# Sums of a softmax's terms: eight blocks on GpSimd, two chains of transfers, no block alone

## The chip, the cores and the metric

The kernel runs on one core of a Trainium2 chip. The metric is the device time of one execution in microseconds (us); smaller is better. A core has engines that run side by side, each working through its own list of instructions in order: TensorE (PE in the profile) multiplies matrices, VectorE (DVE) and ScalarE (ACT) work element by element, GpSimd (POOL) does too and also issues transfers (DMA) that can add to their destination, and SyncE (SP) issues plain transfers. They wait for each other through semaphores. TensorE writes into PSUM; the other tiles here lie in SBUF, or in DRAM.

## The reference

The input is x, 8 images of 2048 tokens with 256 channels, and an adjacency matrix of 2048 x 2048. A graph attention layer with 8 heads of 32 channels is followed by normalizations and a small two-layer network:

```
scores = einsum('fnhd,fmhd->fhnm', q, k) / sqrt(D)
scores = where(adj > 0, scores, -1e9)
attn   = softmax(scores, axis=-1)
t      = einsum('fhnm,fmhd->fnhd', attn, v)
x1 = layernorm(x + t);  x2 = layernorm(x1 + relu(x1 @ w1 + b1) @ w2 + b2)
out = layernorm(x + x2)
```

For every query and head the softmax needs one denominator, the sum of exp(score) over the 2048 keys. How that sum is formed is what the change is about.

## The kernel before

The attention is tiled by image f (8), chunk qc of 512 queries (4), half g of the heads (2 halves of 4 heads), and block mb of 128 keys (16). One (f, qc, g) is a **group**; there are 64, counted from 0 in this text, so an image has eight. One block is an **item**, 1024 in all, and the main loop has one **step** per item.

For an item, `scores` makes the products of keys and queries on PE (line 223) in PSUM, DVE adds the mask and writes the tile `p` (line 226), and ACT takes the exponential in place (line 228). A tile `p` has 128 keys on its partitions and 4 heads x 512 queries along its rows, 1 MB. `values` multiplies it with the values on PE (line 240), summing over the group's 16 blocks in PSUM.

The denominators need a sum over all keys, across the 16 tiles and across the partitions. The partitions are summed by a product with a matrix of ones on PE in `denominator` (line 294), four products, one for each head, per tile: a *set*. To have fewer sets, tiles are first added to each other in `add_up`, called after `values` in each step:

- the blocks of `POOLED` are added on GpSimd into the first of them (line 260);
- the blocks of each chain in `MOVED` are added into the chain's first by a transfer that accumulates, issued by GpSimd (line 257). Each such transfer reads and writes the chain's first tile and so waits for the one before it in its chain;
- the block `ALONE` is added to nothing.

Then `denominator` makes a set for each remaining tile (four), all into one PSUM bank, copies the sum to SBUF on ACT as `dT` (line 296), turns it on PE (line 301) and takes the reciprocal on DVE. Before line 301 the copy has to be done, and ACT gets to it in the order of its list.

The tiles `p` come from a pool of 10 buffers (`bufs=10`). A tile's buffer is free after its last reader: the add or transfer that consumes it, or for a chain's first the ones-products. A buffer freed longest ago is the next to be taken.

The order of the work is written out by hand; nothing is reordered by a planner. In step t the loop first calls `advance`, then issues the scores of item t+2 (`LEAD` is 2), then values and `add_up` of item t:

```
if mb:
    advance(t, 1)
...
    scores(items[t + LEAD])
values(items[t])
add_up(items[t])
if mb == LAST:
    start(t + SUM, denominator(f, qc, g), t)
```

`advance` runs the other work, held as generators in a list sorted by a due time; each `yield BANK` needs a free PSUM bank, and one bank is given per step (none at block 0). `denominator` starts `SUM` = 4 steps after its group's last block, that is in block 3's step of the next group. It has a `yield BANK` before its first set and another one ahead of the set n == 2, so that sets 0 and 1 are made in block 3's step and the rest in block 4's. After that come the turn of dT and, for g = 1, the output's tail (`outcome`, `tail`): normalizations (`norm`, with four small operations on POOL, lines 271 to 275, and four on ACT, line 278), the two-layer network (lines 352 and 362), four adds and multiplications of the whole tile on POOL (lines 344, 346, 367, 369), and two accumulating transfers of x issued by POOL (lines 328 and 371).

POOL's list holds, in this order within a step: the tail's operations that `advance` issues, and then the step's add or transfer.

Of the kernel before, what the change touches and what calls it, by code (L numbers as in the profile page):

```python
# [20 lines left out]
D = 32  # L21
# [32 lines left out]
def fast_path(ctx, tc, cst, x, adj, out, RS):  # L54
    nc = tc.nc
# [29 lines left out]
    def bank(dt=F32):  # L85
        shape = [P, CH] if dt == F32 else [P, 2, CH]
        if state["side"] is not None:
            i = 1 - state["side"]
            return ps_x[i].tile(shape, dt, name=f"x{i}")
        i = state["turn"]  # L90
        state["turn"] = (i + 1) % 5
        pool = ps_s[i] if i < 3 else ps_x[i - 3]
        return pool.tile(shape, dt, name=f"s{i}" if i < 3 else f"x{i - 3}")
# [119 lines left out]
    PT, O, OT, RC = {}, {}, {}, {}  # L213
# [31 lines left out]

    POOLED = (0, 3, 6, 8, 11, 13, 15)
    MOVED = ((1, 4, 7, 10), (2, 5, 9, 12))
    ALONE = 14  # L250
    SUM = 4

    def add_up(item):
        f, qc, g, mb = item
        for chain in MOVED:
            if mb in chain[1:]:
                nc.gpsimd.dma_start(PT[f, qc, g, chain[0]], PT.pop(item), accum_op=ALU.add)  # L257
        if mb in POOLED[1:]:
            first = PT[f, qc, g, POOLED[0]]
            nc.gpsimd.tensor_tensor(first, first, PT.pop(item), ALU.add)  # L260
# [22 lines left out]

    def denominator(f, qc, g):
        grp = (f, qc, g)
        terms = [PT.pop((f, qc, g, ALONE))] + [PT.pop((f, qc, g, chain[0])) for chain in MOVED + (POOLED,)]
        yield BANK
        ps = bank()
        for n, term in enumerate(terms):
            if n == 2:  # L290
                yield BANK
            for h in range(4):
                r = D * h
                nc.tensor.matmul(ps[r:r + D, :], cst["ones"], term[:, h, :], start=(n == 0), stop=(n == 3))  # L294
        dT = op.tile([P, CH], F32, name="dT")
        nc.scalar.copy(dT, ps)
        yield 1
        yield BANK
        ps = bank()
        for j in range(TPC):  # L300
            nc.tensor.transpose(ps[:, j * P:(j + 1) * P], dT[:, j::TPC], ident)
        if g == 0:
            RC[f, qc] = op.tile([P, TPC, H], F32, name="rc")
        rc = RC[f, qc]
        den = ps.rearrange("p (j c) -> p j c", c=P)[:, :, ::D]
        nc.vector.reciprocal(rc[:, :, 4 * g:4 * g + 4], den)
        nc.vector.tensor_tensor(RS[:, 0], RS[:, 0], den, ALU.add)
        nc.vector.tensor_tensor(RS[:, 1], RS[:, 1], den, ALU.min)
        if g == 1:
            begin = items.index((f, qc, g, LAST)) + SUM + 2  # L310
            start(begin, outcome(f, qc), begin)

    def outcome(f, qc):
        yield ROOM
        state["tails"] += 1
        rc = RC.pop((f, qc))
        xin = x[f, qc * CH:(qc + 1) * CH, :].rearrange("(p j) c -> p j c", p=P)
        y = yp.tile([P, TPC, C], F32, name="y")
        for gg in range(2):
            oT = OT.pop((f, qc, gg))  # L320
            yield BANK
            ps = bank()
            for j in range(TPC):
                nc.tensor.transpose(ps[:, j * P:(j + 1) * P], oT[:, j::TPC], ident)
            nc.vector.tensor_tensor(y[:, :, gg * P:(gg + 1) * P].rearrange("p j (h d) -> p j h d", d=D),
                                    ps.rearrange("p (j h d) -> p j h d", h=4, d=D),
                                    rc[:, :, 4 * gg:4 * gg + 4, None].to_broadcast([P, TPC, 4, D]), ALU.mult)
        nc.gpsimd.dma_start(y, xin, accum_op=ALU.add)
        begin = items.index((f, qc, 1, LAST)) + SUM + 2
        start(begin + 10, tail(f, qc, y, xin), begin + 26)  # L330
# [49 lines left out]
    def start(t, gen, due):  # L380
        fill.append([t, gen, 1, due])
        fill.sort(key=lambda e: e[3])
# [72 lines left out]
    for t, (f, qc, g, mb) in enumerate(items):  # L455
        if mb == 0 and t:
            state["side"] = 1 - state["side"]
        if f == 0 and g == 0 and mb == 0 and qc + 1 < NCK:
            start(t, mask_ahead(qc + 1), t + 28)
        if g == 1 and mb == 0 and (f or qc == NCK - 1) and (f + 1 < F or qc + 1 < NCK):  # L460
            load_mask(f + (qc + 1) // NCK, (qc + 1) % NCK)
        if f + 1 < F:
            for what, *which in NEXT.get((2 * qc + g, mb), []):
                due = t + MB // 2 if what is turn else items.index((f + 1, 0, which[1], which[0] * TPC)) - LEAD - 1
                start(t, what(f + 1, *which), due)
        if mb:
            advance(t, 1)
        if t + LEAD < len(items):
            nf, _, ng, nmb = items[t + LEAD]
            t0 = t  # L470
            while (nf, nmb // TPC, ng) not in V:
                advance(t0, 1)
                t0 += 1
# [5 lines that stand above are left out]
# [129 lines left out]
def kernel(  # L608
# [56 lines left out]
    nc.gpsimd.memset(RS[:, 1], 1.0)  # L665

    fast_path(tc, cst, x, adj, out, RS)


# [49 lines left out]
```

## Time and profile before

| | us |
|---|---|
| median of 3 runs | 3730.4 (3729.24 to 3743.26) |
| the profiled execution's own time | 3733.92 |
| its span, first to last instruction | 3732.1 |
| PE busy | 3241.8 (87%) |
| DVE busy | 2760.8 (74%) |
| POOL busy | 2599.1 (70%) |
| ACT busy | 2411.0 (65%) |
| 16 DMA engines, GpSimd's queue | 58.1% of the span |

Line numbers (L294) are those of the kernel before. In lists of groups a row gives line, engine, operation, output<-inputs, how often, then the busy time in all, the mean of one in ns, the idle time of the engine just before it and what ended that. In the timeline a row gives the start, the length, engine, line, operation, and in brackets the idle time before it with what ended it. A matrix product in f32 leaves two records, so a set of four products leaves 8. A POOL record often overlaps the next one's start.

### The profile page before, as it was taken

How to read it: one execution, taken by the hardware profiler on the slowest of the kernel's cores; microseconds unless marked ns; L12 is line 12 of the kernel's file. 1: busy time of each engine (PE TensorE's matmuls, PEld its weight loads, DVE VectorE, ACT ScalarE, POOL GpSimd, SP SyncE). 2: the span in 40 equal slices, each digit the busy share in tenths (PEclk: the TensorE clock that was granted, in tenths of full speed). 3: DMA queues.
4: the chain of work that ended last, by engine and by line, in shares of the span. 5: the costliest groups of instructions: out<-in, count | busy, mean ns of one | idle time of the engine just before them, and what ended most of it. 6: DMA issues, size and time to landing. Idle time of an engine off the chain costs nothing. (4 is left out here: it accounts for less than half of the span.)

```text
span 3732.1 us, 53786 instructions
## 1 busy us (share of the span) xinstructions
PE 3241.8 (87%) x22020; PEld 1038.8 (28%) x22020; DVE 2760.8 (74%) x3203; ACT 2411.0 (65%) x1921; POOL 2599.1 (70%) x1363
## 2 busy tenths in 40 slices
PE   7877888899988899889998899889898889988884
PEld 4222223222322233222332223222232222322221
DVE  4777766877688766788677777777768877688883
ACT  3554555766667666766666776666666676677663
POOL 2555666777677775877667785777777777687775
PEclk9998999999999999999999999999999999999997
DMA  6766675776766775776766776676676676676664
GB/s 185 175 142 152 146 175 117 168 162 142 173 150 145 158 171 145 169 153 154 169 138 151 163 172 158 140 165 154 147 175 141 148 171 152 154 164 140 139 134 86
DMA packets 113774, 573.31 MB, mean 154 GB/s; under 512 B 10833, under 2 KB 27729, under 8 KB 60273
## 3 DMA queue, kind: packets, MB, share of 16 engines
q0 software_dynamic: 64848, 436.90, 58.1%
q1 hardware_dynamic: 47856, 131.61, 10.0%
q8 instruction: 174, 2.85, 0.3%
q10 hardware_dynamic: 816, 1.31, 0.1%
q14 instruction: 80, 0.65, 0.0%
HBM read 129.37 MB, written 37.75 MB: 45 GB/s over the span
## 5 line engine op out<-in xcount | busy, mean ns | idle before, releaser
L226 DVE TENSOR_TENSOR p<-s,mask 128x1024 f32<-128x1024 f32 x2048 | 2410.3, 1219 | 753.8 <-PE s L223 480.0
L228 ACT ACTIVATE p<-p 128x2048 f32<-128x2048 f32 x1024 | 1957.1, 1911 | 1232.9 <-DVE p L226 916.2
L260 POOL TENSOR_TENSOR p<-p 128x2048 f32<-128x2048 f32 x384 | 1835.9, 4810 | 653.6 <-ACT p L228 645.0
L223 PE MATMUL s<-qT,kT 32*128 32x512 f32 x8192 | 1193.2, 652 | 232.5 <-DVE p L226 231.0
L240 PE MATMUL x<-p,v 128*32 128x512 f32 x8192 | 1112.2, 616 | 0.0
L257 POOL DMA_DIRECT2D p<-p x384 | 382.7, 1018 | 351.2 <-ACT p L228 138.9
L223 PEld LDWEIGHTS s<-qT,kT 32*128 32x128 f32 x8192 | 325.3, 186 | 853.6 <-DVE p L226 695.6
L240 PEld LDWEIGHTS x<-p,v 128*32 128x32 f32 x8192 | 162.3, 108 | 795.2 <-issue 645.1
L180 PE MATMUL x<-in,wqkv 128*128 128x512 f32 x472 | 234.6, 620 | 23.1 <-ACT oT L244 10.2
L278 ACT ACTIVATE y<-y,nb,rs 128x256 f32<-128x256 f32 x384 | 224.9, 589 | 38.0 <-POOL nb L275 38.0
L294 PE MATMUL x<-p,ones 128*32 128x512 f32 x2048 | 246.3, 599 | 1.8 <-DVE y L364 0.9
L267 DVE BATCH_NORM_STATS2 st<-y 128x6 f32<-128x256 f32 x384 | 160.1, 417 | 27.1 <-DMA y<-in_x_dram 27.1
L362 PE MATMUL x<-w2s,hT 128*128 128x256 f32 x512 | 127.6, 392 | 45.7 <-ACT oT L244 42.3
L352 PE MATMUL x<-turned,w1s 128*128 128x512 f32 x256 | 128.8, 626 | 20.8 <-ACT hT L353 19.5
L180 PEld LDWEIGHTS x<-in,wqkv 128*128 128x128 f32 x472 | 80.3, 190 | 186.1 <-issue 69.8
L362 PEld LDWEIGHTS x<-w2s,hT 128*128 128x128 f32 x512 | 92.1, 190 | 112.0 <-ACT oT L244 68.6
L205 PE MATMUL x<-wqkv,in 128*128 128x128 f32 x896 | 114.9, 282 | 6.4 <-ACT kT L182 6.3
L205 PEld LDWEIGHTS x<-wqkv,in 128*128 128x128 f32 x896 | 104.2, 192 | 55.0 <-ACT kT L182 34.0
L364 DVE TENSOR_TENSOR y<-x,y 128x512 f32<-128x512 f32 x64 | 44.3, 692 | 94.9 <-PE x L362 94.7
L294 PEld LDWEIGHTS x<-p,ones 128*32 128x32 f32 x2048 | 64.0, 111 | 165.8 <-issue 129.7
L272 POOL TENSOR_TENSOR rs<-rs,mhalf 128x4 f32<-128x4 f32 x96 | 99.3, 1035 | 8.0
L341 PE MATMUL x<-ident,y 128*128 128x128 f32 x256 | 48.0, 299 | 54.5 <-ACT turned L342 38.8
(87 smaller groups left out, 1427.1 us busy)
## 6 DMA issues: line engine op xcount, KB each, us to landing
p<-p POOLq DMA_DIRECT2D x384, 1024.0 KB, 9.7
y<-in_x_dram POOLq DMA_DIRECT2D x64, 512.0 KB, 6.1
in<-xd SPq DMA_DIRECT2D x59, 512.0 KB, 8.0
mask<-md SPq DMA_DIRECT2D x28, 1024.0 KB, 6.6
out_dram<-y SPq DMA_DIRECT2D x32, 512.0 KB, 3.0
in<-in_x_dram SPq DMA_DIRECT2D x28, 512.0 KB, 6.9
xd<-in SPq DMA_DIRECT2D x28, 512.0 KB, 10.0
in<-in_adj_dram SPq DMA_DIRECT2D x24, 512.0 KB, 7.6
```

The lines of the kernel that those rows point to most:

```text
L180: nc.tensor.matmul(ps, wqkv[:, a, k0:k0 + P], xT[:, a, :], start=(a == 0), stop=(a == 1))
L205: nc.tensor.matmul(ps[:, j * P:(j + 1) * P], xT[:, a, j * P:(j + 1) * P], wqkv[:, a, 2 * C + g * P:2 * C + (g + 1) * P], start=(a == 0), s ...
L223: nc.tensor.matmul(ps2[half][:, j, :], KT[f, mb // TPC, g][r:r + D, (mb % TPC) * P:(mb % TPC + 1) * P], QT[f, qc, g][r:r + D, :], start=Tr ...
L226: nc.vector.tensor_tensor(pt[:, 2 * half:2 * half + 2, :], ps, MK[f, qc][:, mb, None, :].to_broadcast([P, 2, CH]), ALU.add)
L228: nc.scalar.activation(pt, pt, AF.Exp, scale=1.0 / math.sqrt(D))
L240: nc.tensor.matmul(O[grp][r:r + D, :], V[f, mb // TPC, g][:, mb % TPC, r:r + D], PT[item][:, h, :], start=(mb == 0), stop=(mb == LAST))
L257: nc.gpsimd.dma_start(PT[f, qc, g, chain[0]], PT.pop(item), accum_op=ALU.add)
L260: nc.gpsimd.tensor_tensor(first, first, PT.pop(item), ALU.add)
L267: nc.vector.bn_stats(st, t[:, j, :])
L278: nc.scalar.activation(t[:, j, :], t[:, j, :], AF.Identity, bias=nb[:, j:j + 1], scale=rs[:, j:j + 1])
L294: nc.tensor.matmul(ps[r:r + D, :], cst["ones"], term[:, h, :], start=(n == 0), stop=(n == 3))
L362: nc.tensor.matmul(ps[:, (j - jj) * C:(j - jj + 1) * C], hT[:, d, j * P:(j + 1) * P], w2s[:, d, :], start=(d == 0), stop=(d == 1))
```

## The change

```diff
-    POOLED = (0, 3, 6, 8, 11, 13, 15)
-    MOVED = ((1, 4, 7, 10), (2, 5, 9, 12))
-    ALONE = 14
+    POOLED = (0, 1, 3, 5, 7, 9, 12, 15)
+    MOVED = ((2, 6, 10, 13), (4, 8, 11, 14))
     SUM = 4
...
     def denominator(f, qc, g):
         grp = (f, qc, g)
-        terms = [PT.pop((f, qc, g, ALONE))] + [PT.pop((f, qc, g, chain[0])) for chain in MOVED + (POOLED,)]
+        terms = [PT.pop((f, qc, g, chain[0])) for chain in MOVED + (POOLED,)]
         yield BANK
         ps = bank()
         for n, term in enumerate(terms):
@@
                 yield BANK
             for h in range(4):
                 r = D * h
-                nc.tensor.matmul(ps[r:r + D, :], cst["ones"], term[:, h, :], start=(n == 0), stop=(n == 3))
+                nc.tensor.matmul(ps[r:r + D, :], cst["ones"], term[:, h, :], start=(n == 0), stop=(n == 2))
         dT = op.tile([P, CH], F32, name="dT")
```

GpSimd makes seven adds in a group instead of six, the first after block 1 instead of block 3. There are still two chains of three transfers each, of other blocks: 6, 8, 10, 11, 13 and 14 are moved instead of 4, 5, 7, 9, 10 and 12. No tile goes to the ones-products by itself: there are three sets instead of four. The order of the sets was block 14, the two chains, GpSimd's sum; now it is the two chains, GpSimd's sum. The `yield BANK` ahead of n == 2 stays, so that two sets are made in block 3's step, now the two chains', and one set in block 4's.

## The prediction

> **What bounds the kernel now.** I read the page first, for engines and costly rows (busy time, share, count; in rows: busy, mean ns of one, idle before it).
>
> ```profile
> PE 3241.8 (87%) x22020; PEld 1038.8 (28%) x22020; DVE 2760.8 (74%) x3203; ACT 2411.0 (65%) x1921; POOL 2599.1 (70%) x1363
> ...
> L260 POOL TENSOR_TENSOR p<-p 128x2048 f32<-128x2048 f32 x384 | 1835.9, 4810 | 653.6 <-ACT p L228 645.0
> ...
> L294 PE MATMUL x<-p,ones 128*32 128x512 f32 x2048 | 246.3, 599 | 1.8 <-DVE y L364 0.9
> ```
>
> PE is the busiest, and the ones-products (L294) are work on it; POOL has 30% idle, mostly waiting for new blocks. That favours the change. But an average says nothing of the two steps concerned, so next came the waits (total us, times, longest).
>
> ```profile
> PE x L301 <- ACT dT L296: 16.5, 63, 0.7
> ...
> POOL p L257 <- DMA p<-p: 111.7, 32, 6.7
> ...
> DVE p L226 <- DMA p<-p: 25.8, 19, 5.0
> ```
>
> In 63 of 64 groups PE already waits for the denominator's copy dT. And POOL stops at transfers that wait for the one before them in their chain. Then the timeline where group 35's denominator is made (start us, length).
>
> ```profile
> 2147.06 1.90 PE L294 MATMUL x<-p,ones 128*32 128x512 f32 x16
> ...
> 2148.84 1.91 ACT L228 ACTIVATE p<-p 128x2048 f32<-128x2048 f32 x1 [2.10 <-DVE p L226]
> ...
> 2148.89 1.14 PE L223 MATMUL s<-qT,kT 32*128 32x512 f32 x8
> ...
> 2149.96 1.07 PE L240 MATMUL x<-p,v 128*32 128x512 f32 x8
> ...
> 2150.65 0.57 ACT L296 COPY dT<-x 128x512 f32<-128x512 f32 x1
> 2151.27 0.75 PE L301 MATMUL x<-ident,dT 128*128 128x128 f32 x4 [0.24 <-ACT dT L296]
> ```
>
> The last ones-products end at 2148.96, yet dT starts at 2150.65: ScalarE, in order, is in the exp of a block whose scores were issued before those products. PE itself waits 0.24 us for dT.
>
> **What the skill says.** GPSIMD Engine Reference, 3.1, gives 4497 ns for a GpSimd add of 2048 f32; the shortest add in this trace is 4498 ns. Trainium Kernel Development and Optimization, Key Constraints: transfers of all queues run on the same 16 engines; here transfers close together land later (below). TensorE: Matmul & The Clock Gate, Part 1: an idle window of about 3.4 us halves PE's clock until it has been busy for such a window. The trace agrees (row: stretch, length, PE busy, ..., clock granted):
>
> ```profile
> 424.00:430.00 6.00, 0.00 (x0) 0.00 (x0) 1.82 (x3) 0.00 (x0) 0.00 (x0) 0.88 0.78 203
> 430.00:435.40 5.40, 5.00 (x20) 1.44 (x21) 4.09 (x5) 3.76 (x4) 2.12 (x1) 0.50 0.00 0
> ```
>
> **Part 1: one set of products less.** A set is 8 records; two sets take 16 records, 1.90 us, and the next matmul starts 1.83 us after the first (2147.06 to 2148.89), so 0.92 us a set and 64 x 0.92 = 59 us of PE work. It is the second step's set that goes (n = 0, 1 stay in one step, n = 2 is alone in the next). Cover: the exp ahead of dT. It ends at 2150.75 whatever the second step's PE does, since its scores were issued at 2145.1, before. So L301 still starts at 2151.27, and PE's 0.24 us wait becomes 1.16. In 62 groups dT starts as that exp ends and about 1.7 us after the products. Gain: 0. Bounds: 0 to 59 us, the latter if the exp moved too. I take 0.
>
> **Part 2: one add more on POOL.** Shortest 4.5, mean 4.81 us: 64 x 4.81 = 308 us, 70% to 78% busy. Block 1's add fills the idle time at a group's start (9.06 us ahead of the first add of group 35). Behind it are the other adds and transfers and norm's four small operations, for which ScalarE's L278 waits, two steps after they are issued; worked through all groups, L278 keeps 4 us or more, outside five cases that have next to nothing today. Cost 0; if all adds were exposed, 308.
>
> **Part 3: where the transfers stand.** Six per group, as before, but blocks 4, 5, 7, 9, 10, 12 become 6, 8, 10, 11, 13, 14. The first products, in block 3's step of the next group, need both chains: block 13's (n = 0), block 14's (n = 1). Before, the last transfer was block 12's, and it went to the second step. The dense stretch of a group is the test; group 36, POOL and then PE:
>
> ```profile
> 2170.98 4.86 POOL L260 TENSOR_TENSOR p<-p 128x2048 f32<-128x2048 f32 x1
> 2175.49 2.65 POOL L367 TENSOR_TENSOR y<-y,g2r 128x1024 f32<-128x1024 f32 x1
> 2177.81 1.18 POOL L257 DMA_DIRECT2D p<-p  x1
> 2178.41 2.98 POOL L369 TENSOR_TENSOR y<-y,be2r 128x1024 f32<-128x1024 f32 x1
> 2180.72 5.17 POOL L260 TENSOR_TENSOR p<-p 128x2048 f32<-128x2048 f32 x1
> 2185.22 1.51 POOL L371 DMA_DIRECT2D y<-in_x_dram  x1
> ...
> 2189.45 1.90 PE L294 MATMUL x<-p,ones 128*32 128x512 f32 x16
> ```
>
> Records overlap, so starts give the cost: add 4.5 us, L367 and L369 2.3, L371 0.8, a transfer's issue 0.6. Transfers: asked one by one, this group's six land 6.8, 9.6, 9.8, 9.7, 9.9 and 7.4 us after issue; landings that queue are 4.9, 5.5 and 4.9 us apart. So 7.0 us alone, 5.0 behind another; for the half-size L328 and L371 behind one I take 2.5 (half the bytes; bounds 0 and 4.3, as L328 after block 5 here).
>
> POOL's new order in group 36, exps as they ended. Block 5's add and norm's operations end at 2157.3: transfer 6 issued, lands 2164.3. Add 7 after L328: to 2164.2; transfer 8: L328 lands 2166.8, this one 2171.8. Add 9 to 2169.3; transfer 10 lands 2176.8. Transfer 11 waits for 8 in its chain: 2171.8, lands 2181.8. L367, add 12, L369: 2.3 + 4.5 + 2.3 on 2172.4, to 2181.5. Transfer 13: 2181.6, though its exp ended at 2174.7; lands 2188.7. L371 lands 2191.2. Transfer 14, issued about 2183, lands 2196.2. PE wants n = 0 at 2189.45 (in time) and n = 1 at 2190.3: it waits 5.9 us. What is late next: scores of block 5 and all behind them. Block 5 also takes block 14's buffer (the pool gives out the one freed longest ago), but PE has waited already. The 25.8 us of buffer waits now at blocks 1 and 3 mostly go; in these groups that only lengthens the new wait.
>
> Working the same table for every group gives a wait in 21: numbers 10, 12, 16, 18, 20 and so on (0, 2 and 4 of an image's eight, and 62), whose last blocks come every 2.55 us without other PE work. Mean 5.2 us, sum 108. In the other groups steps are near 4 us and transfer 14 lands 4 us or more early.
>
> **Part 4: the clock.** In the trace every PE gap above 3 us (ten, ahead of the last group's tail) is followed by 3.4 to 6.4 us at half clock, as in the rows above. After the new wait the products n = 1 (0.92 us) and the scores (1.1) run at half speed ahead of the exp that dT needs: 2.0 us; later work hides in the 0.92 us slack of part 1. 21 x 2.0 = 42 us; bounds 0 and 21 x 3.4.
>
> **Sum.** 0 + 0 + 108 + 42 = 150 us on a span of 3732.1 is 3882. The profiled execution took 3733.9, 1.8 over its span and 3.5 over the median of 3730.4; on the median, 3880.
>
> **Rivals.** (a) Faster: the exp moves up with PE, and transfer 14 lands in time. For it: PE 87% busy, no idle time before L301 but 0.24 us. Against it: dT starts 1.7 us after the products. 3730 - 59 = 3671. It decides only if block 14's transfer lands by 2190.3, 13 us after its exp. (b) No change: transfer in time, gain lost before dT: 3730. It takes L371 and transfer 13 not standing ahead of 14; even without L371's 2.5 us the wait is 3.4. (c) POOL bounds everything, all adds exposed: 3730 + 308 = 4038. Against it: 22% would still be idle. (d) Inside my forecast: shorter waits (2.9 us, 1 us of clock: 82, so 3812) or longer (8 us, 2.5 us: 220, so 3950).
>
> **Chances.** Forecast with (d) 0.83, (c) and other losses 0.04, (b) 0.07, (a) 0.06. About 0.5% is what a measurement of this kernel tells from no change. Range 3790 to 3955: (d)'s ends, the lower one widened for fewer late groups.
>
> **What would show it.** PE waiting in L294 for the transfer p<-p about 21 times, 4 to 7 us each, in the odd groups' fourth step; PE clock below 1 after them; L301's wait for dT near 1.2 us elsewhere; POOL near 78% of the old span; dense groups as long as before, the groups after them 5 to 9 us longer. I am wrong if L294 never waits, or if L301 starts 0.9 us earlier after its exp.

## The result, and the profile after

The changed kernel took 3971.9 us (median of 4 runs, 3963.1 to 3977.5) against 3734.3 us for the kernel before (4 runs): a ratio of 1.063, 95% interval 1.060 to 1.066. The prediction was 3880, with a range of 3790 to 3955. The direction and the place of the loss were as predicted; its size was not: the trace has 242 us where the prediction's sum had 150, and the range's upper end was missed by 17 us. The profiled execution took 3976.5 us, its span 3974.2, which is 242.0 over the span before. In the changed kernel all lines from 256 to 370 have a number one lower than before (L294 is now L293, L257 L256, L260 L259, L371 L370). The kernels of the experiments have numbers of their own.

The page's rows of the changed kernel, as shown of the kernel before: engines first, then groups (busy in all, mean ns of one, then the idle time before it and what ended it).

```profile
PE 3250.6 (82%) x21508; PEld 1026.7 (26%) x21508; DVE 2778.4 (70%) x3203; ACT 2409.5 (61%) x1921; POOL 2884.5 (73%) x1427
...
L259 POOL TENSOR_TENSOR p<-p 128x2048 f32<-128x2048 f32 x448 | 2106.5, 4761 | 730.4 <-ACT p L228 676.7
...
L293 PE MATMUL x<-p,ones 128*32 128x512 f32 x1536 | 219.8, 667 | 179.8 <-DMA p<-p 177.6
```

512 records of products are gone, yet PE is busy 9 us longer: products at half clock take twice the time. POOL has its 64 adds more and is still idle for 27% of the longer span. And the ones-products, which had 1.8 us of idle time ahead of them in all, now have 179.8, nearly all ended by a transfer. The waits (total us, times, longest) say how often:

```profile
PE x L293 <- DMA p<-p: 177.6, 45, 7.1
...
DVE p L226 <- DMA p<-p: 91.6, 43, 4.3
POOL p L256 <- DMA p<-p: 83.3, 25, 6.8
...
PE x L300 <- ACT dT L295: 58.7, 58, 1.6
```

The first line did not exist before. The second is VectorE's wait for a free buffer; it was 25.8 in 19 waits, the third 111.7 in 32, the last 16.5 in 63. Next the timeline where group 36's denominator is made, the group that the prediction worked through (start us, length, engine, line; in brackets the idle time before it):

```profile
2304.87 1.06 PE L240 MATMUL x<-p,v 128*32 128x512 f32 x8
...
2307.33 1.06 PE L293 MATMUL x<-p,ones 128*32 128x512 f32 x8 [1.40 <-DMA p<-p]
...
2307.41 2.35 DVE L226 TENSOR_TENSOR p<-s,mask 128x1024 f32<-128x1024 f32 x2 [1.99 <-DMA p<-p]
...
2314.70 1.93 PE L293 MATMUL x<-p,ones 128*32 128x512 f32 x8 [6.30 <-DMA p<-p]
2316.56 2.09 PE L223 MATMUL s<-qT,kT 32*128 32x512 f32 x8
2318.58 1.94 PE L240 MATMUL x<-p,v 128*32 128x512 f32 x8
```

Set n = 0 waits 1.40 us for block 13's transfer and set n = 1 another 6.30 us for block 14's. VectorE waits for block 13's landing too: block 4 of the new group gets the buffer that this transfer reads, and its mask add starts 0.1 us after the landing. What follows on PE runs at half speed: scores take 2.09 us where 1.14 is usual, values 1.94 instead of 1.07. The stretches of the same place (stretch, length, then PE, PEld, DVE, ACT and POOL busy, the clock granted, DMA engines' busy share, GB/s):

```profile
2306.50:2314.70 8.20, 1.07 (x9) 0.16 (x9) 2.87 (x4) 2.31 (x2) 8.12 (x2) 0.76 0.94 192
2314.70:2320.60 5.90, 5.90 (x28) 1.31 (x32) 1.82 (x2) 0.00 (x0) 2.45 (x5) 0.50 0.00 0
```

For 8.2 us PE works 1.07 us and the transfer engines 94% of the time: PE waits for bytes on their way. Then PE is busy throughout and has half its clock. POOL's list of the same group shows where those transfers came from:

```profile
2273.29 0.93 POOL L256 DMA_DIRECT2D p<-p  x1 [0.31 <-ACT p L228]
...
2280.02 1.19 POOL L256 DMA_DIRECT2D p<-p  x1
...
2285.12 1.53 POOL L256 DMA_DIRECT2D p<-p  x1
2289.19 0.86 POOL L256 DMA_DIRECT2D p<-p  x1 [2.55 <-DMA p<-p]
2289.75 2.69 POOL L366 TENSOR_TENSOR y<-y,g2r 128x1024 f32<-128x1024 f32 x1
2292.08 4.88 POOL L259 TENSOR_TENSOR p<-p 128x2048 f32<-128x2048 f32 x1
2296.60 2.67 POOL L368 TENSOR_TENSOR y<-y,be2r 128x1024 f32<-128x1024 f32 x1
2298.89 1.21 POOL L256 DMA_DIRECT2D p<-p  x1
2299.57 1.43 POOL L370 DMA_DIRECT2D y<-in_x_dram  x1
2300.12 1.76 POOL L256 DMA_DIRECT2D p<-p  x1
```

The six L256 are blocks 6, 8, 10, 11, 13 and 14, in the predicted order. The tile's view of the last two gives their time from issue to landing:

```profile
DMA to landing us min/median/max: 8.4/11.5/14.5
```

Block 13's took 8.4 us, block 14's, third in a queue with L370, 14.5. Neither was issued soon after its exp: in the 21 groups that the prediction lists, block 13's transfer was issued 10.0 us and block 14's 8.7 us after it in the mean, because the tail's operations and the adds stand ahead of them in POOL's list (block 12's before: 6.9 us in the same groups).

**Where the 242 us are.** I took the start of the values in each of the 1024 steps in both traces, gave each step the time up to the next start, and subtracted. Up to the first values +3.1; then, for all groups but the last, blocks 0 and 1 +32.0, blocks 2 to 5 +217.5 and blocks 6 to 15 -31.6; the last group with its tail +21.0. In blocks 2 to 5, in which the denominator of the group before is made, the 20 groups that follow a predicted late group (all 21 but the last one, 62) have +211.3, 10.6 us each, and the other 42 that follow a group together +3.3, their median 0.00 (group 0 has +2.8). Group 62's denominator, made in the last group, costs another 9.4. So 221 of the 242 us come from the denominators of exactly the 21 groups that the prediction lists.

### The profile page after: what moved, and what is told of

Read it like the earlier page. It is cut to its first block, busy times and chain, and to the rows that moved or that the text cites. A ratio compares the mean times of both kernels' runs of the same rounds, so it can differ in the third digit from the quotient of the medians.

```text
span 3974.2 us, 53011 instructions
## 1 busy us (share of the span) xinstructions
PE 3250.6 (82%) x21508; PEld 1026.7 (26%) x21508; DVE 2778.4 (70%) x3203; ACT 2409.5 (61%) x1921; POOL 2884.5 (73%) x1427
## 5 line engine op out<-in xcount | busy, mean ns | idle before, releaser
L259 POOL TENSOR_TENSOR p<-p 128x2048 f32<-128x2048 f32 x448 | 2106.5, 4761 | 730.4 <-ACT p L228 676.7
L223 PE MATMUL s<-qT,kT 32*128 32x512 f32 x8192 | 1209.9, 660 | 242.3 <-DVE p L226 240.2
L256 POOL DMA_DIRECT2D p<-p x384 | 400.8, 1059 | 213.6 <-ACT p L228 107.0
L293 PE MATMUL x<-p,ones 128*32 128x512 f32 x1536 | 219.8, 667 | 179.8 <-DMA p<-p 177.6
L293 PEld LDWEIGHTS x<-p,ones 128*32 128x32 f32 x1536 | 44.8, 117 | 330.6 <-DMA p<-p 223.4
L300 PE MATMUL x<-ident,dT 128*128 128x128 f32 x256 | 48.1, 310 | 58.9 <-ACT dT L295 58.7
```

The lines of the kernel that those rows point to most:

```text
L223: nc.tensor.matmul(ps2[half][:, j, :], KT[f, mb // TPC, g][r:r + D, (mb % TPC) * P:(mb % TPC + 1) * P], QT[f, qc, g][r:r + D, :], start=Tr ...
```

## The experiments

In what follows "late groups" are those 20 (in which a late sum is used), "the other groups" the other 42, and a gain or loss of theirs is that of the four steps of blocks 2 to 5, against the profiled execution before. "All groups" leaves out the last. Ratios are to runs of the kernel before on the same chip. The traces are from several chips, on which the kernel before took 3734 to 3744 us in the median; a difference of a few us between two traces says little.

### Is a set worth nothing because it leaves the second step?

Both kernels are the kernel before with block 14 left out of the sum, so that three sets remain. They differ in where the second step begins.

```diff
-        terms = [PT.pop((f, qc, g, ALONE))] + [PT.pop((f, qc, g, chain[0])) for chain in MOVED + (POOLED,)]
+        PT.pop((f, qc, g, ALONE))
+        terms = [PT.pop((f, qc, g, chain[0])) for chain in MOVED + (POOLED,)]
...
             if n == 2:            # the first kernel; n == 1 in the second
```

> The kernel before with block 14 left out of the denominators: three sets of ones-products, the set taken away is the second step's; adds and transfers as before, the early ones. Theory (the set taken from the second step is hidden, because the copy dT stands behind an exp whose scores were issued before it): no change, 3734 us within 15, and the wait of the turn L301 for dT grows from 0.24 to about 1.16 us a group. Rival (the products are work on the busiest engine, so they count): 64 x 0.92 = 59 us less, 3675.

> The same, block 14 left out of the denominators, but with one set in the first step and two in the second. Theory: the scores of block 5 and the exp ahead of dT move up by one set, 0.92 us in each of 64 groups, 3675 us, and the wait for dT stays near 0.24 us. Rival (the second step's gain is lost elsewhere, in VectorE or ScalarE, and not at dT): no change, 3734.

With two sets in the first step, one in the second (one set less in the second): 3723.9 us, ratio 0.995 (0.994 to 0.997), and blocks 2 to 5 of all groups are +0.7 us in total. With one and two (one set less in the first): 3690.5 us, ratio 0.988 (0.985 to 0.990), blocks 2 to 5 are -48.4 us. The wait for dT in the first kernel and then in the second:

```profile
PE x L302 <- ACT dT L297: 71.6, 64, 1.6
```

```profile
PE x L302 <- ACT dT L297: 22.6, 64, 1.5
```

The set taken from the second step went whole into that wait: 16.5 before, 71.6 now. The set taken from the first step moved the scores, their exp and dT with it, 0.84 us in a median group. So for this step part 1's price of zero was right, and the reason for it too. The first kernel's runs are still half a per cent faster, 19 us in the median. The trace doesn't show where: its span is only 3.9 us shorter than before, with 7.4 us less in blocks 6 to 15 and 5.7 more ahead of the first values. This stays open.

### Is it block 14's transfer, or POOL's load?

The changed kernel with block 14 left out of its chain, and so of the sum:

```diff
     def add_up(item):
         f, qc, g, mb = item
+        if mb == 14:
+            PT.pop(item)
+            return
```

> The changed kernel with block 14's transfer left out, and so block 14 left out of the denominators; seven adds on GpSimd and three sets stay. Theory (the late transfer of block 14 is the cost): PE waits only for block 13's transfer, 1 to 2 us in 21 groups, with little loss of clock: 3735 to 3785 us. Rival (GpSimd's seventh add sets the pace): 3900 or more.

3788.4 us, ratio 1.013 (1.011 to 1.015). All eight blocks are still summed on GpSimd, so the eighth block by itself is not what costs 240 us: the rival, 3900 or more, falls. The time is 3 us over the theory's 3785; the wait that it expected is there:

```profile
PE x L296 <- DMA p<-p: 37.0, 21, 3.2
```

Those are the sums of the 21 groups, 1.8 us each, now behind block 13's transfer, which the prediction had in time. The late groups lose 2.3 us instead of 10.6. So block 14's transfer accounts for 8.3 us of 10.6 and block 13's alone for 2.3. What the work ahead of the two in POOL's list has in their lateness, this run leaves as it was.

### What does the transfer of x add that stands between them?

The changed kernel without the last x transfer; the output then lacks the last addition of x.

```diff
         nc.gpsimd.tensor_tensor(z, z, rows(cst["be2r"]), ALU.add)
         yield 1
-        nc.gpsimd.dma_start(z, xin, accum_op=ALU.add)
         yield 7
```

> The changed kernel with the tail's last transfer (x added to z, line 370) left out, so the output lacks x; nothing else differs. Theory (the transfers of blocks 13 and 14 share the engines with it, in one queue): block 14 lands 2.5 to 3 us earlier in the 21 groups, and PE waits about 5.5 us there instead of 8.2; with the tail's end some 6 us shorter, about 3900 us. Rival (block 14 is late by its own issue and its own 14 us, whatever lies ahead of it): the waits as long as in the changed kernel, 3960 us or more.

3897.1 us, ratio 1.041 (1.039 to 1.043), as expected; the late groups lose 7.2 us, and PE waits 5.1 us in each of the 21 sums instead of 8.2. The waits of this kernel, and the landing of its group 36's transfers 13 and 14:

```profile
PE x L293 <- DMA p<-p: 110.4, 41, 6.0
```

```profile
DMA to landing us min/median/max: 7.3/9.1/10.9
```

Block 14's transfer lands 3.6 us sooner after its issue (10.9 for 14.5). This has two parts: 2.5 us is the queueing of half a transfer, as the prediction had it, and 1.1 us is block 13's own transfer, which takes 7.3 us instead of 8.4. In this group all else is the same in both kernels: block 11's transfer has 0.7 us left when block 13's is issued, and block 14's is issued 1.2 or 1.3 us behind it; L370, 0.7 us behind it, is in the changed kernel alone. Over all 21 groups block 13's transfer took 8.4 us in the mean in the changed kernel, 8.3 in the kernel without block 14's transfer, and 7.3 here. So the x transfer lengthens the one that it follows.

### Would another order of the sets have helped?

GpSimd's sum first, so that block 14's chain comes into the second step:

```diff
-        terms = [PT.pop((f, qc, g, chain[0])) for chain in MOVED + (POOLED,)]
+        terms = [PT.pop((f, qc, g, chain[0])) for chain in (POOLED,) + MOVED]
```

> The changed kernel with GpSimd's sum as the first set, so that block 14's chain comes in the second step, 3.8 us later. Theory with the buffer (block 5 takes block 14's buffer, so VectorE waits for the same landing): only about 3 us of the 10.5 us a group are won, 3734 + 180 = about 3910 us, with VectorE waiting for the transfer in its mask add. Rival (only the products wait): 6 us or more a group are won, about 3840 us.

3902.9 us, ratio 1.043 (1.041 to 1.045); the late groups lose 7.1 us. The waits:

```profile
DVE p L226 <- DMA p<-p: 192.8, 66, 5.4
...
PE x L293 <- DMA p<-p: 90.9, 23, 4.8
...
PE x L293 <- POOL p L259: 24.4, 20, 2.3
```

One step more of time buys 3.5 us of 10.6. PE's wait for transfers is halved, with 24.4 us for GpSimd's sum beside it, and DVE's wait for buffers doubles, 91.6 to 192.8: block 5 gets the buffer that block 14's transfer reads. In all 21 cases its mask add starts 0.1 us after that landing; these waits are 101.0 us. So the late transfer has two customers, and giving one of them more time brings out the other.

The other way to give time is the split, one set in the first step and two in the second (`if n == 1:`), with the sets in the order of the change:

> The changed kernel with one set in the first step and two in the second, blocks as in the change. Theory: 0.85 us won in the 42 groups where no transfer is late (36 us); in the 21 others block 14 is wanted a step later, but VectorE waits for the same landing for block 5's buffer, so about 7 us a group stay: 3734 + 160 - 36 = about 3860 us. Rival (only the products' wait counts): about 4 us a group, 3790 us.

3873.5 us, ratio 1.035 (1.033 to 1.037): the other groups win 0.83 us each, as in the second kernel of the first pair, and the late groups lose 7.8. DVE waits for buffers 190.5 us, as in the run before, 100.2 of them in block 5's mask add for block 14's landing. The theory holds.

### Would earlier chains cure it?

The form of the change with all transfers done by block 13:

```diff
-    POOLED = (0, 1, 3, 5, 7, 9, 12, 15)
-    MOVED = ((2, 6, 10, 13), (4, 8, 11, 14))
+    POOLED = (0, 1, 5, 7, 9, 12, 14, 15)
+    MOVED = ((2, 4, 8, 11), (3, 6, 10, 13))
```

> The changed kernel with other blocks: GpSimd adds 1, 5, 7, 9, 12, 14, 15 into 0; the chains are 2, 4, 8, 11 and 3, 6, 10, 13. Seven adds, six transfers, three sets, two of them in the first step, as in the change. Theory (only the place of the last transfers costs): no wait for a transfer in the products, and no gain from the set taken from the second step: 3715 to 3745 us. Rival (seven adds cost by themselves, or three sets gain 59 us): above 3780, or 3675.

And the same with the split at n == 1:

> The same blocks, and one set in the first step, two in the second. Theory: the gain of the kernel with one set in the first step, 50 us, without leaving any block out: 3670 to 3695 us. Rival (block 15's add or block 13's transfer is late for the second step): 3720 or more, with PE waiting in the products.

3791.7 us, ratio 1.013 (1.011 to 1.015), and 3774.1 us, ratio 1.009 (1.007 to 1.010). Both are far better than the change, and both missed what I expected by 45 to 80 us. The late groups still lose 2.1 and 2.3 us. The waits of the first kernel, then the one of the second that is left (PE's for transfers is 1.1 us there, once):

```profile
DVE p L226 <- DMA p<-p: 85.1, 43, 3.7
...
PE x L293 <- DMA p<-p: 23.4, 20, 2.2
```

```profile
DVE p L226 <- DMA p<-p: 89.2, 43, 5.0
```

The split gives PE the time for block 13's transfer, and the late groups gain nothing by it: in all 21 cases block 4's mask add waits for the buffer that this transfer reads, 54.7 us in all in the first kernel and 54.8 in the second. So the late landing of block 13's transfer costs some 2 us a group through the buffer, whether the products wait for it or not. My theories had nothing for this wait. Blocks 0 and 1 lose 30 and 32 us, as in the change, and blocks 6 to 15 win 26 and 25.

The first kernel's time is also above the 3780 that I had named for the rival that seven adds cost by themselves. The trace speaks against it: of the 49 us of blocks 2 to 5 the late groups have 42, and the other 42 groups, with the same adds, 3.4. But in the 21 groups block 13's transfer is issued 10.0 us after its exp, as in the change; what part the adds ahead of it have in that was not taken apart.

### The old chains, with block 14 in GpSimd's sum

This leaves the transfers where they were before and makes block 14 an eighth term of GpSimd's sum, three sets in all.

```diff
-    POOLED = (0, 1, 3, 5, 7, 9, 12, 15)
-    MOVED = ((2, 6, 10, 13), (4, 8, 11, 14))
+    POOLED = (0, 3, 6, 8, 11, 13, 14, 15)
+    MOVED = ((1, 4, 7, 10), (2, 5, 9, 12))
```

> The changed kernel with the transfer chains of the kernel before: (1, 4, 7, 10) and (2, 5, 9, 12) stay, and block 14 joins GpSimd's sum: (0, 3, 6, 8, 11, 13, 14, 15). Three sets, the third in the second step. Theory (it is the place of the last two transfers that costs, not the eighth add nor the missing set): no wait in L293 for a transfer worth more than 20 us in total, blocks 0-1 as before; three adds in a row (13, 14, 15, 4.5 us each at steps of 2.55 us) let block 15's add end about 1.8 us after PE wants it in some 20 groups, so 3730 to 3770. Rival (the eighth add holds POOL's transfers back wherever it stands): L293 waits for transfers in the same 21 groups by 2 us or more, 3790 or more.

> The kernel of the run before this one, but with one set in the first step and two in the second. Theory (a set taken from the first step lets the exp ahead of dT start 0.8 us earlier, a set taken from the second step doesn't): 0.84 us less in each of some 44 groups in which nothing waits for the sum, 35 to 50 us below that run, so 3685 to 3725, and below the kernel before. Rival (the two sets of the second step run into the wait for dT or for block 15's add, and the gain goes into that): within 10 us of that run.

3818.1 us, ratio 1.020 (1.017 to 1.022), and with the split 3784.5 us, ratio 1.012 (1.009 to 1.014), both well over what I expected. The waits for the sum's products in the first of them:

```profile
PE x L293 <- POOL p L259: 61.6, 22, 4.6
PE x L300 <- ACT dT L295: 48.8, 44, 1.6
```

The products no longer wait for a transfer, so the rival, that the eighth block holds the transfers back wherever it stands, is refuted, though the time lies in its range of 3790 or more. The late groups lose 3.4 us to a new wait: 2.8 us each, where I had estimated 1.8, for the adds of blocks 13, 14 and 15, which queue on POOL. Here the eighth block does cost, by its place at the end of the sum. With the clock that follows, the time is 48 us over the upper end of the theory. Blocks 0 and 1 are back at -2.2 us (+32.0 in the change); that loss came with the new blocks of the chains (below, under Buffers). The split wins 34 us on the medians (35 to 50 expected below the run without it), 0.85 us in each of the other groups.

### Block 14 in a chain of five

The last pair makes GpSimd's sum what it was and puts block 14 at the end of the first chain, with the split at n == 1 and that chain last. In the first kernel of the pair the last x transfer also goes two steps later, behind block 15's add.

```diff
-    POOLED = (0, 1, 3, 5, 7, 9, 12, 15)
-    MOVED = ((2, 6, 10, 13), (4, 8, 11, 14))
+    POOLED = (0, 3, 6, 8, 11, 13, 15)
+    MOVED = ((2, 5, 9, 12), (1, 4, 7, 10, 14))
...
+        terms = [PT.pop((f, qc, g, chain[0])) for chain in (MOVED[0], POOLED, MOVED[1])]
...
+            if n == 1:
...
-        yield 1
+        yield 3
         nc.gpsimd.dma_start(z, xin, accum_op=ALU.add)
```

> The kernel before with block 14 put behind block 10 in the first chain: chains (2, 5, 9, 12) and (1, 4, 7, 10, 14), GpSimd's sum as before (seven adds less one, no eighth), three sets, chain 2 alone in the first step, then the sum and the chain of five; the last x transfer two steps later, behind block 15's add. Theory (only what lands late costs, and a set taken from the first step gains 0.84 us a group): transfer 14 is issued behind block 13's add, 8 us after its exp in the dense groups, lands 7 to 8.4 us later, as the third set wants it: 0 to 1.5 us lost in 21 groups, 0.84 won in most, 3690 to 3730. Rival (a transfer of block 14 is late wherever it stands, since its exp is one step from the end): 3 us or more in 21 groups, 3770 or more.

> The same kernel with the last x transfer where it was, just ahead of block 14's transfer. Theory (landings queue, 2.5 us for half the size): block 14 lands 2 to 3 us later than in the run before this one in the dense groups, the third set waits that long and its clock falls: 40 to 80 us above that run, 3735 to 3800. Rival (the transfer has slack there, or what lands ahead of it costs it nothing): within 15 us of that run.

3753.5 us, ratio 1.003 (1.002 to 1.004), with the x transfer later; 3821.3 us, ratio 1.020 (1.017 to 1.023), with it where it was. In group 36 of the first, block 14's transfer is issued 8.0 us after its exp and lands 7.7 us later, as expected, and the products do not wait. In the second kernel, with L370 issued 0.6 us ahead of it, it lands 10.7 us after issue, 3.0 us more, and the waits are back:

```profile
DVE p L226 <- DMA p<-p: 131.1, 42, 6.5
...
PE x L293 <- DMA p<-p: 65.9, 22, 4.1
```

The 67.8 us between the two are inside the expected 40 to 80: a transfer of half the size, moved by two steps, is worth that here. The first kernel itself missed its 3690 to 3730. Its late groups lose 1.0 us, inside the 0 to 1.5 of the theory, but the other groups win only 0.5 us instead of 0.84, and the last group with its tail is 13.6 us longer. DVE's waits for buffers do not explain the first: of their 59.7 us 56 lie in groups after a late one. The second kernel, with the x transfer where it was, wins 0.88 us in the other groups, so the loss came with the later x transfer or with what follows it. How, and what lengthened the tail, was not taken apart. None of the kernels that compute the whole sum is faster than the kernel before.

An eleventh buffer for `p`, which would take away some of the buffer waits and so measure them directly, was not tried.

## Why the prediction was right or wrong, step by step

**Part 1, the set removed: 0. Right.** The wait for dT rose from 16.5 to 71.6 us where only that set was taken away from the second step, and the steps concerned stayed at +0.7 us in total; the 19 us by which its runs are faster nevertheless lie elsewhere and are not explained. The alternative bound, 59 us, belongs to a set taken from the first step, which gave 48.4. In the changed kernel the wait for dT was 1.1 us in the median of the other groups, for 1.16 predicted.

**Part 2, the seventh add: 0. Right, as far as was tested.** POOL was busy 2884.5 us, 73% of the new span, which is 77% of the old one (78% predicted), the other 42 groups had +3.3 us in all, and leaving block 14's transfer out brought most of the time back with all the adds in place. Rival (c), 4038, is refuted with it.

**Part 3, the late transfers: the failed step.** The groups were right, all 21, and so was the order of POOL's list in group 36. The wait was mis-sized: 5.2 us predicted in the mean, 8.2 measured (1.9 ahead of n = 0 and 6.3 ahead of n = 1). The step that failed is block 13's landing, which the prediction had in time for n = 0, 0.75 us ahead of it in group 36. From there to block 14's landing it had 7.5 us, and 7.4 was measured (the median of the 21), so that the error lies in block 13's landing and in what leads up to it. The term is the 7.0 us for a transfer with nothing ahead of it. I applied it whatever came behind. In the trace of the changed kernel, block transfers with nothing ahead of them land 6.9 us (median of 23) after issue where another block's is issued within 2 us behind, as I had it; but 8.0 (26 of them) where a half-size x transfer is issued 1 to 2 us behind, and 8.4 (14) where it is within 1 us. In the trace before no such transfer was followed by one of x within 2 us, so it did not show this.

In each of the 21 groups this happens twice: block 6's transfer, with L327 behind it, took 8.0 us in the mean, and block 13's, with L370 behind it, 8.4. In group 36, counted from the same exps, transfer 11 was issued 1.8 us later than in my table: 1.0 of this is block 6's slower landing, which held up L327 and block 8's behind it, 0.4 that transfer 6 was issued later, and 0.5 the time from block 8's landing to the issue of transfer 11, for which I had nothing. Transfer 13, behind it on POOL, was issued 1.7 us later, and its own landing took 8.4 instead of 7.1. In sum block 13's landed 3 us late against my table, and so did block 14's. PE came to n = 0 there 0.9 us later as well, so that the group's wait grew less, from 5.9 to 7.7. The table of the other groups is not on record, and how their 3 us divide is open. That block 13's would be "in time" failed with all this: alone it costs 2.3 us a group.

**Buffers.** I wrote that the buffer waits at blocks 1 and 3 would mostly go. They did (19.3 of the 25.8 us stood there), but others came, and the landings at which they end tell which. In groups after a late sum, block 2's mask add waits for transfer 11 (28.1 us in 19 waits) and block 4's for transfer 13 (57.6 us in 21); each starts 0.1 us after that landing. The prediction named block 5 and block 14's buffer, which came out in the run with the other order, and had nothing for block 4. Of the 32 us lost at blocks 0 and 1, 23 lie in these groups; with the old chains the loss is absent (-2.2 us). Of the 31.6 us won at blocks 6 to 15, 22.8 lie in block 15's step of the 21 groups, in 14 of which block 1's mask add had waited for transfer 10 before. In the time the two cancel out.

**Part 4, the clock: 2.0 us predicted.** What is left of 10.5 us a group after the wait of 8.2 is 2.3. The Trainium skill, TensorE: Matmul & The Clock Gate, Part 1, which the prediction drew on, agrees with the stretches shown in that half clock, for 5.9 us, follows a wait of 6.3. But its idle window of about 3.4 us is longer than what the trace needed: gaps near 2 us had half clock behind them too (last section), and there the measurement decides. That the 2.3 us are all due to the clock was not tested apart.

**The sum.** 21 x 8.2 = 172 and 21 x 2.3 = 48 make 220 in place of 150. The last group and its tail add some 12 us beyond group 62's denominator, 5 of them PE's wait for the last group's own transfers; that I had not counted. The remaining 10 us are the start and small differences in other steps. Of the 92 us that the sum lacked, the wait is thus 64, the clock 6, the last group 12 and the rest 10. My rival (d) with its longer waits (8 us and 2.5 us) was what happened, without the last group: 3950.

## What to carry to other kernels

A transfer's time from issue to landing has to be read together with what is issued behind it, not only ahead of it: take the duration of one with the same neighbours on both sides, where the trace has one. When accumulating transfers are shifted to later blocks, first find the earliest consumer of the last one and count back from it (exp, place on the issuing engine, queue); then list the second consumer, here the next owner of each buffer that a late transfer reads, because it takes over the wait when the first gets more time. And before pricing removed work, ask in which step it stands: the same ones-products were worth 0 in one step and 0.84 us a group in the step before it.

## What the runs showed of the hardware

A transfer of 1 MB that accumulates from one tile into another and has nothing ahead of it took 6.9 us (median) in the changed kernel with another such transfer issued within 2 us behind it, but 8.0 or 8.4 us with an accumulating one of 512 KB from DRAM there. Taking this one away brought block 13's transfer from 8.4 to 7.3 us in the mean of 21 groups. I had expected a later one to wait its turn. Why the two kinds differ was not tested.

Half clock followed shorter gaps than I had assumed. In the trace of the kernel before, from 350 us on to ahead of the tail, none of 88 idle gaps of PE between 1.2 and 1.8 us was followed by half clock within 12 us, 12 of 16 between 1.8 and 2.2 us were, and all 7 longer ones. (Ends of matmuls are modelled, so a gap may really be longer than it looks.) In the change half clock came to 400 us of the span, 170 before.
